# A two-layer graph network on one core: half of a dense pass replaced by gathered rows and small products

## The chip, the core and the metric

The kernel runs on one core of one Trainium2 chip, in single precision. The engines named below are TensorE (PE; its weight loads are a row of their own, PEld), VectorE (DVE), ScalarE (ACT), GpSimd (POOL) and SyncE (SP), whose queue issues most of the plain DMAs. POOL issues the indirect DMAs: one of them reads 128 row numbers from a column of an integer tile and fetches 128 rows of a DRAM table into the 128 partitions. The metric is the time of one execution on the device in microseconds; of several runs the median is given. A profile is one execution of its own, with a time span that starts at its first instruction and ends at its last.

## The reference, cut to what matters

Two layers over a graph of 3,327 nodes with 512 features each. The adjacency matrix `adj` (3,327 x 3,327) is sparse: node weights fall like one over the square root of the index, so the first rows and columns are the fullest, and the last hold a few entries in a hundred or fewer. Cut to its core:

```python
# layer 0
h = relu(layernorm(x))
u = h @ W1                      # 512 -> 128
g = relu(adj @ u + b1)          # first pass over adj
x = x + adj @ (g @ W2) + b2     # second pass: (adj @ g) @ W2
# layer 1
h = relu(layernorm(x))
t = adj @ h                                         # both sums run over the neighbours
s = exp(-leaky_relu(s_left[:, None] + s_right[None, :], 0.01)) * (adj != 0)
x_a = (s / s.sum(1)) @ (h @ W_sa)                   # attention
x_b = t @ W_gcnb + b_gcnb
own_a, own_b = h @ Wa_self + ba, h @ Wb_self + bb   # a node's own logits
x = x + sigmoid(sigmoid(t @ Wa + own_a) * x_a + sigmoid(t @ Wb + own_b) * x_b)
```

`s_left` and `s_right` are products of h with two vectors made of W_sa and a_sa. In the kernel a block's own logits are `node[i][:, 1:3]`, and its `s_left` is `node[i][:, 0:1]`.

## The kernel before, in words

Rows are padded to 3,328: 26 blocks of 128 nodes (`NB`). Seven chunks of columns of the transposed adjacency matrix (`chunks`): six of 512 and one of 256.

**First pass** (lines 493 to 537). For each chunk, 26 tiles of 128 x 512 of the adjacency matrix are loaded on SP's queue, and PE adds up `acc_u` (line 512). A product of single precision is two instructions in the profile. Beside each, DVE takes the largest magnitude of every group of 32 columns (line 516). From these, `make_lists` (line 382) writes for every block which rows of the matrix have any entry in a group of 32 columns: `row_h` holds node numbers, `row_a` row numbers of the table `adj_groups`, whose rows are 32 neighbouring columns. `list_rooms` says how many list places a block has: none for block 0, 9 for block 1, down to 5 for blocks 6 to 10, 4 for 11 to 18, 3 for 19 to 25. A place is 128 row numbers for two groups at once, and each block has two such halves: 228 columns of row numbers in all. As lists come up, `gather_adj` (line 148) fetches the pieces of the adjacency matrix into the tiles `ae`, one indirect DMA of 128 rows of 128 bytes for each column, each held back by a product that it is paced to (`gather_behind`). `make_g` ends a chunk: g of four blocks, kept in SBUF.

**Second pass** (lines 678 to 724). The same tiles are loaded again and `acc_g` is added up over all blocks of g (line 685). After a chunk, `make_h1` (line 579) makes for each of its blocks the product with W2 (`px`), the new x, its layer norm, h with its score as a row of 520 numbers (`hrow`, twelve of them in turn), the two scores (line 563), the own logits (line 567) and the store into the DRAM table `h_rows`. Block 0 is the hub, too full for lists: `add_hubs` adds up its two sums over all 26 h blocks, 52 products (line 644), beside the later chunks and after the last.

**Layer 1** (lines 767 to 987). Blocks 25 down to 1 by lists: `attend` (line 776) gathers rows of h (2,080 bytes) by `row_h` on POOL, makes the attention weights on DVE and ACT; `sums` (line 816) adds up 64 x 64 products over the gathered rows, `turn` transposes, `weigh` multiplies by the weights, `finish` (line 739) adds all up and stores. A block's gathers are paced to the sums of the third or fourth block before it (`LEAD`). If a list has no room for all rows (`overflow`), a dense path after it computes layer 1 anew; with these inputs it isn't taken.

The order on each engine is that of a scheduler at build time, by the order in the program, by readiness and by the marks `queued`, `issue_after` and `high_priority`; at run time every engine and queue runs in that order.

Of the kernel before, what the change touches and what calls it, by code (L numbers as in the profile page):

```python
# [27 lines left out]
WAKE = 14  # L28
LN_EPS = 1e-5
# [17 lines left out]
def kernel(  # L47
# [23 lines left out]
    NCH = len(chunks)  # L71
# [37 lines left out]
    s_left = [kept([P, CW // P, 2 * GW], f"s_left{c}") for c in range(NCH)]  # L109
    s_hub = kept([P, P], "s_hub")  # L110
    x1_dram = [dram.tile([P, D], F32, tag=f"x1_{i}", name=f"x1_{i}") for i in range(NB)]
    h_dram = dram.tile([NP, ROW], F32, tag="h_rows", name="h_rows")

# [16 lines left out]
    NR = 12  # L130
    rows = [
        hubp.tile([P, 2, ROW], F32, tag=f"rows{k}", name=f"rows{k}", bufs=1) for k in range(NR // 2)
    ]
    hrow = [t[:, k, :] for t in rows for k in range(2)]
    for t in rows:
        nc.vector.memset(t[:, :, D:], 0.0)

    def gather(dst, table, rows, last):
        return nc.gpsimd.indirect_dma_start(  # L139
            out=dst, out_offset=None, in_=table,  # L140
            in_offset=bass.IndirectOffsetOnAxis(ap=rows, axis=0),
            bounds_check=last, oob_is_err=False,
        )

    adj_groups = adjT.rearrange("j (b i) -> (j b) i", i=GW)
    listed = set()

    def gather_adj():

        for i in range(1, NB):  # L150
            r = rooms[i]
            for k0, k1 in segments(i):
                for q in range(2):
                    for k in range(k0, k1):
                        while (i, q) not in listed:
                            yield None
                        f = first[i] + q * r + k
                        yield gather(
                            ae[i][:, 2 * k0 + q * (k1 - k0) + k - k0, :GW], adj_groups,
                            row_a[:, f : f + 1], NP * NG - 1,  # L160
# [55 lines left out]
    with (  # L216
# [5 lines left out]
        def load_adj(j, c, name, n=1):  # L222

            c0, w = chunks[c]
            n = min(n, NB - j)
            t = adjp.tile([P, CW], F32, tag="adj", name=f"{name}_{c}_{j}")
# [33 lines left out]
        g = [l0.tile([P, HID], F32, tag=f"g{i}", name=f"g{i}") for i in range(NB)]  # L260
# [8 lines left out]
        def normalize(i):  # L269

            hs[i] = l0w.tile([P, D], F32, tag="h", name=f"h_{i}", bufs=3)
# [24 lines left out]
        def make_g(c, acc):  # L296

            c0, w = chunks[c]
            gT = l0w.tile([HID, CW], F32, tag="gT", name=f"gT_{c}")
            relu = nc.scalar.activation(gT[:, :w], acc[:, :w], AF.Relu, bias=b1_col)  # L300
            pg = bank(psB, f"pg_{c}")
            for b in range(w // P):
                nc.tensor.transpose(pg[:, b * P : (b + 1) * P], gT[:, b * P : (b + 1) * P], ident)
            for b in range(w // P):
                nc.vector.tensor_copy(g[c0 // P + b], pg[:, b * P : (b + 1) * P])
# [76 lines left out]
        def make_lists(c, most):  # L382


            c0, w = chunks[c]
            g0, n = c0 // GW, w // GW

            def small(shape, name, dtype, bufs=2):
                return l0w.tile(shape, dtype, tag=name, name=f"{name}_{c}", bufs=bufs)
# [18 lines left out]
            p_off = bank(psB, f"p_off_{c}")  # L408
# [9 lines left out]
            step = steps[c % 2]  # L418
            p_sh = bank(psB, f"p_sh_{c}")
# [14 lines left out]
            for batch in batches:  # L434
# [19 lines left out]
                for i, q in batch:  # L454
# [18 lines left out]
                nc.vector.tensor_scalar(  # L473
                    row_h[:, f0 : f0 + m], jb[:, :m], float(NP - 1), None, op0=ALU.min
                )
# [17 lines left out]
        for c in range(NCH):  # L493
            c0, w = chunks[c]
            acc = bank(psA, f"acc_u_{c}")
            per = CW // w
            most = l0w.tile([P, MG, NB], F32, tag="most", name=f"most_{c}")
            for j in range(NB):
                if c == 0:
# [8 lines left out]
                if j % per == 0:  # L508
                    with queued(x_loaded[min(j + 4, NB - 1)] if c == 0 else None):
# [5 lines left out]
                with queued(scaled[min(j + 3, NB - 1)] if c == 0 else None):  # L515
# [6 lines left out]
                if j % 3:  # L522
                    gather_behind(added)
                if c == 0 and j % 2 == 0:
# [6 lines left out]
            with tc.issue_after(chunk_end.ins):  # L531
                if c == 1:
                    load_weights()
                if 0 < c <= HUB_LOADS:
                    load_hub(c - 1)
            lists = make_lists(c, most)
# [3 lines left out]
        for s in range(2):  # L540
            a_row = l0w.tile([P, D], F32, tag="h", name=f"a_row_{s}", bufs=3)
# [12 lines left out]
            nc.vector.tensor_copy(w_rows[:, s, :], pw)  # L554

# [11 lines left out]
        def own_logits(i, junk):  # L567

            for s in range(2):
                nc.vector.scalar_tensor_tensor(  # L570
                    junk, hrow[i % NR][:, :D], 1.0, w_own[:, s, :], op0=ALU.mult, op1=ALU.mult,
                    accum_out=node[i][:, 1 + s : 2 + s],
                )
# [543 lines left out]
```

## Time and profile before

Three runs: 844.13, 844.46 and 846.61 us, median 844.46. The profiled execution's span is 840.2 us, 4.3 us below the median; around the span lies the start and end of the program.

| Engine | Busy us | Share of the span | Instructions |
|---|---|---|---|
| PE | 781.6 | 93% | 3,615 |
| PEld | 416.9 | 50% | 3,615 |
| DVE | 515.6 | 61% | 1,658 |
| ACT | 187.6 | 22% | 396 |
| POOL | 493.4 | 59% | 513 |

The first-pass products run from 11 to 220 us, those of the second pass from 220 to 434, the hub's last sums end at 457, and from 458 on layer 1 runs. In a group of the profile the columns are: busy us, mean ns of one; idle time of the engine just before them, and what ended most of it. "Issue" is a wait that the profile names no cause for. In a timeline a row is start, duration, engine, line, operation, tiles, and in brackets the idle time of the engine before it.

### The profile page before, as it was taken

The numbers are of one execution on the slowest core, as the hardware profiler recorded it, in microseconds if no ns is written. First come the engines' busy times: TensorE is split into PE (matmuls) and PEld (weight loads), VectorE is DVE, ScalarE is ACT, GpSimd is POOL, SyncE is SP. The second block draws the span as 40 slices with busy tenths as digits, with TensorE's granted clock in tenths as the row PEclk, the third lists the DMA queues.
The fourth block names the chain that finished last, engine by engine and source line by source line (L and its number), as shares of the span: only waits on it lengthen the run. The fifth ranks groups of instructions, "written<-read, shape, count | busy, mean of one in ns | idle before, by whom it ended". The sixth has DMA issues, their size and how long they took to land.

```text
span 840.2 us, 12143 instructions
## 1 busy us (share of the span) xinstructions
PE 781.6 (93%) x3615; PEld 416.9 (50%) x3615; DVE 515.6 (61%) x1658; ACT 187.6 (22%) x396; POOL 493.4 (59%) x513
## 2 busy tenths in 40 slices
PE   9999899999799999999999599799998999999795
PEld 7774344445443444444464366455554555454363
DVE  7778989999646866685775455345535353443342
ACT  7770000000002313033052022122222222121121
POOL 3202756676677777776716555666766767667400
PEclk9999999999799999999999799899999999999798
DMA  8787998898578989998958556787788867777600
GB/s 272 242 292 227 330 283 262 285 299 276 151 236 297 368 281 306 319 343 284 345 180 260 158 182 196 216 227 217 225 225 215 228 203 227 207 210 209 187 26 30
DMA packets 106891, 200.14 MB, mean 238 GB/s; under 512 B 16801, under 2 KB 30656, under 8 KB 106816
## 3 DMA queue, kind: packets, MB, share of 16 engines
q1 hardware_dynamic: 72592, 124.40, 45.2%
q0 software_dynamic: 25536, 63.74, 27.9%
q10 hardware_dynamic: 8688, 11.15, 3.8%
q8 instruction: 30, 0.49, 0.2%
q14 instruction: 45, 0.37, 0.1%
HBM read 179.39 MB, written 20.55 MB: 238 GB/s over the span
## 4 chain that ended last, share of the span: by engine, by line
PE 66%; issue 18%; DMA 7%; DVE 5%; another core or an unknown queue 3%; ACT 1%; SPq 0%; ACTq 0%; DVEq 0%
PE acc L829 14%; PE p_b L883 12%; PE p_a L890 11%; PE acc_g L685 10%; PE acc_u L512 5%; PE acc_hub L644 3%; DMA a<-in_adjT_dram 3%; PE ptt L843 3%; PE pu L291 3%; PE px L587 2%; DMA W_sa_sb<-in_W_sa_dram 1%; PE pt L283 1%; DMA xb<-in_x_dram 1%; DVE junk L563 1%
## 5 line engine op out<-in xcount | busy, mean ns | idle before, releaser
L139 POOL DMA_INDIRECT ae<-in_adjT_dram,row_a x228 | 246.4, 1081 | 151.6 <-issue 57.8
L139 POOL DMA_INDIRECT hr<-h_rows,row_h x140 | 144.1, 1029 | 64.5 <-issue 30.8
L685 PE MATMUL acc_g<-a,g 128*128 128x512 f32 (+1 forms) x364 | 160.3, 575 | 5.7 <-DMA a<-in_adjT_dram 3.8
L512 PE MATMUL acc_u<-a,rows 128*128 128x512 f32 (+1 forms) x364 | 159.9, 578 | 2.8 <-DMA a<-in_adjT_dram 2.2
L139 POOL DMA_INDIRECT rows<-h_rows,row_h x88 | 90.7, 1031 | 69.2 <-DVE e_hub L206 20.3
L883 PE MATMUL p_b<-W_g_sb,tyT 128*128 128x257 f32 x416 | 102.0, 395 | 16.3 <-issue 15.7
L516 DVE TENSOR_REDUCE most<-a 128x16 f32<-128x512 f32 (+1 forms) x182 | 110.6, 638 | 6.1 <-DMA a<-in_adjT_dram 5.2
L685 PEld LDWEIGHTS acc_g<-a,g 128*128 128x128 f32 x364 | 67.0, 192 | 85.5 <-issue 61.1
L883 PEld LDWEIGHTS p_b<-W_g_sb,tyT 128*128 128x128 f32 x416 | 78.3, 193 | 48.5 <-issue 19.3
L890 PE MATMUL p_a<-W_sa_sb,tyT 128*128 128x512 f32 (+2 forms) x216 | 97.5, 590 | 3.5 <-issue 3.1
L512 PEld LDWEIGHTS acc_u<-a,rows 128*128 128x128 f32 x364 | 66.5, 194 | 58.7 <-issue 51.9
L829 PE MATMUL acc<-hr,ae 64*64 64x512 f32 x560 | 81.7, 612 | 3.2 <-issue 2.3
L858 DVE COPY tyT<-ptt 128x512 f32<-128x512 f32 x51 | 34.9, 686 | 54.2 <-PE acc L829 21.8
L890 PEld LDWEIGHTS p_a<-W_sa_sb,tyT 128*128 128x128 f32 x216 | 41.1, 193 | 47.1 <-issue 45.6
L208 DVE SCALAR_TENSOR_TENSOR ae<-ae 128x192 f32<-128x192 f32 (+2 forms) x36 | 12.5, 368 | 79.1 <-issue 29.9
L829 PE MATMUL acc<-rows,ae 64*64 64x512 f32 x352 | 49.0, 607 | 1.7 <-issue 1.4
L829 PEld LDWEIGHTS acc<-hr,ae 64*64 64x64 f32 x560 | 30.9, 137 | 39.2 <-issue 37.9
L748 ACT ACTIVATE f<-f 128x2 f32<-128x2 f32 x26 | 5.3, 203 | 166.9 <-DVE f L747 118.4
L300 ACT ACTIVATE gT<-acc_u,b_col 128x512 f32<-128x512 f32 (+1 forms) x7 | 4.6, 657 | 157.1 <-issue 101.3
L563 DVE SCALAR_TENSOR_TENSOR junk<-rows,w_rows 128x512 bf16<-128x512 f32 x52 | 35.7, 686 | 3.0 <-issue 0.5
L716 DVE TENSOR_TENSOR xb<-xb,b_row 128x512 f32<-128x512 f32 x26 | 17.7, 689 | 30.4 <-DMA xb<-in_x_dram 19.6
L843 PEld LDWEIGHTS ptt<-ident,ty 128*128 128x128 f32 x208 | 24.5, 144 | 19.1 <-issue 18.2
(142 smaller groups left out, 907.5 us busy)
## 6 DMA issues: line engine op xcount, KB each, us to landing
a<-in_adjT_dram SPq DMA_DIRECT2D x338, 256.0 KB
h_rows<-rows SPq DMA_DIRECT2D x26, 260.0 KB
x<-in_x_dram SPq DMA_DIRECT2D x26, 256.0 KB
xb<-in_x_dram SPq DMA_DIRECT2D x26, 256.0 KB
x<-xb ACTq DMA_DIRECT2D x26, 256.0 KB
x1b<-x SPq DMA_DIRECT2D x26, 256.0 KB
out_dram<-va SPq DMA_DIRECT2D x25, 256.0 KB
ae<-in_adjT_dram,row_a POOLq DMA_INDIRECT x228
```

Of the source, the lines that this page charges most:

```text
L139: return nc.gpsimd.indirect_dma_start(out=dst, out_offset=None, in_=table, in_offset=bass.IndirectOffsetOnAxis(ap=rows, axis=0), bounds_ch ...
L291: nc.tensor.matmul(pu[:, :HID], hT[:, k, :], W1_sb[:, k, :], start=(k == 0), stop=(k == KD - 1))
L512: added = nc.tensor.matmul(acc[:, :w], u[j], a[:, :w], start=(j == 0), stop=(j == NB - 1))
L516: nc.vector.tensor_reduce(most[:, : w // GW, j], a[:, :w].rearrange("p (b i) -> p b i", i=GW), axis=AX.X, op=ALU.max, apply_absolute_value ...
L563: return nc.vector.scalar_tensor_tensor(junk, h, 1.0, w_rows[:, s, :], op0=ALU.mult, op1=ALU.mult, accum_out=into)
L644: nc.tensor.matmul(acc_hub[k], s, hrow[i % NR][:, :D], start=(i == 0), stop=(i == NB - 1))
L685: added = nc.tensor.matmul(acc[:, :w], g[j], a[:, j % per, :], start=(j == 0), stop=(j == NB - 1))
L829: added = nc.tensor.matmul(taken[i]["acc"][h][q * HALF : (q + 1) * HALF, :], both[half_p, q * n + k, :], taken[i][k0][k][half_p, q, :D], s ...
L843: moved = nc.tensor.transpose(pt[:, k * P : (k + 1) * P], ty[h][:, k * P : (k + 1) * P], ident)
L858: last = nc.vector.tensor_copy(dst, src)
L883: nc.tensor.matmul(p_b[n][:, :WH], tyT[:, k, 0, :], W_g_sb[:, k, n * WH : (n + 1) * WH], start=(k == 0), stop=(k == KD - 1),)
L890: last = nc.tensor.matmul(p_a[:, c0:c1], tyT[:, k, 1, :], W_sa_sb[:, k, c0:c1], start=(k == 0), stop=(k == KD - 1),)
```

## The change

- **Order of the first pass.** Chunks are taken from the last columns to the first (`back`): six of 512, then the 256 of blocks 0 and 1. The lists follow that order.
- **Second pass.** The last three chunks of 512, blocks 14 to 25 (`listed_chunks`), get no dense products. Their sums come from the lists: g is also stored to a DRAM table (`g_dram`), 82 indirect DMAs fetch 128 rows of 128 numbers each (`gather_g`), into four tiles of four list columns that are used in turn, and `list_sums` multiplies the pieces in `ae` by them, 64 x 32 by 64 x 128, into two PSUM banks per chunk; a copy, a transpose and a copy give sT. Blocks 0 to 13 stay dense, three chunks of 512 and one of 256 (`dense_chunks`), and the steps at which list sums are put between their products are written out (`SUMS`).
- **Making h.** `make_h1` calls for up to three of four steps instead of every second; blocks are made in the order of `made_order`, dense and listed chunks in turn; the loads of x come block by block; the hub's sums are asked for from the second dense chunk on, at every third step.
- **Own logits.** They leave the second pass. In layer 1 each block's h is loaded again (256 KB on SP's queue), and the three DVE instructions follow its `attend`.
- **Gathers of the adjacency matrix.** They follow two of three steps in both passes (one of three in the half-wide last chunk of the first); those left after the second pass are issued in layer 1, five after the gathers of each block (`AE_PER`).
- **Bounds.** No indirect DMA has a bounds check now; the lists' row numbers are clamped before `row_a` is made, which adds one small copy per batch.
- **Overflow path.** It also computes anew the listed blocks of layer 0; this code is left out below.

```diff
-    def gather(dst, table, rows, last):
+    def gather(dst, table, rows):
         return nc.gpsimd.indirect_dma_start(
             out=dst, out_offset=None, in_=table,
             in_offset=bass.IndirectOffsetOnAxis(ap=rows, axis=0),
-            bounds_check=last, oob_is_err=False,
         )
...
-                nc.vector.tensor_scalar(
-                    row_h[:, f0 : f0 + m], jb[:, :m], float(NP - 1), None, op0=ALU.min
-                )
+                nc.vector.tensor_scalar(jb[:, :m], jb[:, :m], float(NP - 1), None, op0=ALU.min)
+                nc.vector.tensor_copy(row_h[:, f0 : f0 + m], jb[:, :m])
...
-            for b in range(w // P):
-                nc.vector.tensor_copy(g[c0 // P + b], pg[:, b * P : (b + 1) * P])
+            gs = l0.tile([P, n, HID], F32, tag=f"g{c0}", name=f"g{c0}")
+            nc.vector.tensor_copy(gs, pg[:, :w].rearrange("p (b f) -> p b f", f=HID))
+            with tc.issue_after(relu.ins):
+                nc.scalar.dma_start(g_dram[c0 : c0 + w, :].rearrange("(b p) f -> p b f", p=P), gs)
...
-                if j % 3:
+                if j % 3 if w == CW else j % 3 == 0:
                     gather_behind(added)
...
+        def gather_g(n):
+            for i, f in g_slots:
+                k = len(g_taken) % NU
+                if not k:
+                    g_tile[0] = l0w.tile([P, D], F32, tag="h", name=f"g_row_{f}", bufs=GR // NU)
+                t = g_tile[0][:, k * HID : (k + 1) * HID]
+                g_taken.append(f)
+                gather(t, g_dram[:, :], row_h[:, f : f + 1])
...
+        def list_sums():
+
+            for k, (c0, w) in enumerate(listed_chunks):
+                acc = [bank(psB, f"acc_s_{c0}_{h}") for h in range(2)]
+                for b, i in enumerate(range(c0 // P, (c0 + w) // P)):
+                    r = rooms[i]
+                    for k0, k1 in segments(i):
+                        for kk in range(k0, k1):
+                            for q in range(2):
+                                t = g_rows.pop(first[i] + q * r + kk)
+                                for h in range(2):
+                                    half_p = slice(h * HALF, (h + 1) * HALF)
+                                    part = slice((2 * h + q) * GW, (2 * h + q + 1) * GW)
+                                    nc.tensor.matmul(
+                                        acc[h][part, b * P : (b + 1) * P],
+                                        ae[i][half_p, 2 * k0 + q * (k1 - k0) + kk - k0, :GW],
+                                        t[half_p, :], start=(kk == 0), stop=(kk == r - 1),
+                                    )
+                    gather_g(2 * r)
+                    yield
...
+    SUMS = (15, 22, 28, 33, 37, 42, 47, 52, 57, 62, 67, 72, 74)
...
-        for c in range(NCH):
+        gather_g(GR)
+        order = [i for c0, w in back for i in range(c0 // P, (c0 + w) // P)]
+        step = 0
+        for c, (c0, w) in enumerate(dense_chunks):
...
+                step += 1
...
+                if step in SUMS:
+                    next(summing, None)
-                if (c * NB + j) % 5 != 4:
+                if step % 3:
                     gather_behind(added)
-                if j % 2:
+                if n % 4 != 3:
...
+    def own_logits(pool, i):
+
+        own_h = pool.tile([P, D], F32, tag="own_h", name=f"own_h_{i}")
+        nc.sync.dma_start(own_h, h_dram[i * P : (i + 1) * P, :D])
...
+        def fetch_ae(n):
+            for _ in range(n):
+                with queued(gathered[0]):
+                    gathered[0] = next(columns, None) or gathered[0]
...
                 for seg in segments(i):
                     made = attend(i, seg)
...
+            with queued(made[0]):
+                own_logits(spw, i)
+            fetch_ae(AE_PER)
```

## The prediction

> **What bounds the kernel now.** I read the page first, then the busy time by stage, then the queue of GpSimd (POOL) in order of time, then one block of the last stage. The page's head and four of its groups (columns: busy us, mean ns of one; idle before, and what ended it):
>
> ```profile
> span 840.2 us, 12143 instructions
> PE 781.6 (93%) x3615; PEld 416.9 (50%) x3615; DVE 515.6 (61%) x1658; ACT 187.6 (22%) x396; POOL 493.4 (59%) x513
> ...
> L139 POOL DMA_INDIRECT ae<-in_adjT_dram,row_a x228 | 246.4, 1081 | 151.6 <-issue 57.8
> L139 POOL DMA_INDIRECT hr<-h_rows,row_h x140 | 144.1, 1029 | 64.5 <-issue 30.8
> L685 PE MATMUL acc_g<-a,g 128*128 128x512 f32 (+1 forms) x364 | 160.3, 575 | 5.7 <-DMA a<-in_adjT_dram 3.8
> L139 POOL DMA_INDIRECT rows<-h_rows,row_h x88 | 90.7, 1031 | 69.2 <-DVE e_hub L206 20.3
> ```
>
> TensorE is busy 93% of the time; POOL looks loose at 59%. By stage (stretch, its length, then busy us of PE, PEld, DVE, ACT, POOL, the clock, the DMA share, GB/s) the cuts are the end of the first tiles, of the first pass, of the second pass's products, of the hub's sums:
>
> ```profile
> 66.00:226.00 160.00, 148.35 (x789) 72.41 (x789) 141.74 (x380) 3.91 (x6) 97.86 (x96) 0.97 0.85 266
> 226.00:435.00 209.00, 202.63 (x528) 90.69 (x526) 142.26 (x468) 53.10 (x102) 148.50 (x132) 0.99 0.91 300
> 435.00:458.00 23.00, 22.03 (x54) 9.61 (x56) 12.29 (x45) 6.12 (x16) 10.18 (x11) 1.00 0.67 227
> 480.00:840.00 360.00, 331.75 (x1801) 186.83 (x1799) 161.45 (x576) 74.97 (x163) 209.73 (x204) 0.97 0.66 189
> ```
>
> PE fills 224.7 of the second pass's 232 us (226 to 458). But POOL's share hides a limit. Its queue in order of time:
>
> ```profile
> 316.57 1.00 POOL L139 DMA_INDIRECT ae<-in_adjT_dram,row_a  x1 [0.30 <-issue]
> 317.87 1.00 POOL L139 DMA_INDIRECT ae<-in_adjT_dram,row_a  x1 [0.30 <-issue]
> 319.17 1.00 POOL L139 DMA_INDIRECT ae<-in_adjT_dram,row_a  x1 [0.30 <-issue]
> ...
> 578.96 1.00 POOL L139 DMA_INDIRECT hr<-h_rows,row_h  x1 [0.30 <-issue]
> ```
>
> A gather takes 1.00 us and the next cannot follow for another 0.30: one per **1.30 us** (about 1.35 with the occasional longer one), the same for 128 bytes per index (ae) as for 2,080 (hr). In the second pass 132 gathers x 1.35 = 178 us of 209: POOL is 85% full, not 71%. Last, PE in a block of the last stage:
>
> ```profile
> 603.87 3.63 PE L829 MATMUL acc<-hr,ae 64*64 64x512 f32 x30
> 607.43 3.74 PE L883 MATMUL p_b<-W_g_sb,tyT 128*128 128x257 f32 x16
> 611.01 3.72 PE L890 MATMUL p_a<-W_sa_sb,tyT 128*128 128x512 f32 x8
> 614.56 1.04 PE L843 MATMUL ptt<-ident,ty 128*128 128x128 f32 x8
> ```
>
> PE runs without a gap: 11.7 us for a block with four list places, 10.8 for one with three (the chain of waits steps 482.1, 493.0, 503.8). A block's gathers (eight, or six) need 10.8 or 8.1 us of POOL.
>
> **What the Trainium skill says.** *DMA: Bandwidth & Descriptors*, "SWDGE vs HWDGE vs iDMA": a GpSimd DMA's descriptors are computed by software on the Q7 cores. The trace agrees: POOL's time follows the index count, not the bytes. *GPSIMD Engine Reference*, "Elementwise — side-by-side cycle accounting": data-dependent branching costs about 12 cycles per element. No run here shows it; used below. *TensorEngine Tiling (Array Packing)*, "Key Properties": tiles work independently, but changing the tiling mode drains the engine. The 30 64x64 products above take 0.121 us each, about a quarter of the 0.43 of a full 512-wide one: they do overlap. *TensorE: Matmul & The Clock Gate*, "The HAM clock gate": PE idle beyond some 3.4 us halves its clock. The trace agrees (458 to 480 us: 12.6 us busy, clock 0.77), so long waits cost twice.
>
> **The change, part by part.**
>
> *Second pass, products.* Chunks go from six and a half to three and a half: 182 products to 104, 78 of 512 columns gone. One is two instructions of 0.43 us (a run of 22 took 9.71), so 78 x 0.86 = **-67 us** of PE. Their 78 loads of 256 KB leave SP's queue and DMA share (0.91) falls; no wait depends on it then.
>
> *Second pass, list sums.* 82 lists (2 x 41 places in blocks 14 to 25) x 2 halves = 164 products of 64 rows, 32 weights, 128 columns: 328 instructions. The trace has none such. Cheapest: columns alone count, a quarter of 0.121, 10 us. Dearest: they run like transposes of 128 columns, 1.04/8 = 0.13, 43 us. I take 0.065, **+21 us**, and +2 for 12 transposes. PE's second pass becomes 224.7 - 67 + 23 = 181 us.
>
> *Second pass, gathers.* POOL gets 82 gathers of g; those of adjacency fall to two steps in three: 70 in 104 steps. They share one queue in order. Beyond the first 16, a g gather waits until PE's sums free its tile; behind it stand adjacency gathers and the next g gathers, for which PE's next sums wait. The last sums stand at step 74: by then POOL has issued 82 + 50 = 132. They start when g of the last first-pass chunk is stored, 229 us.
>
> *Bounds check.* All gathers lose their bounds check (its register move runs under the gather before and costs nothing). Its price inside the 1.00 us is shown nowhere. Bounds: nothing (1.30 stays) to all of it (0.30 left). The time is per index, and a compare with a possible skip is per-index work; 12 cycles x 128 at the skill's 1.2 GHz would be 1.28 us, more than all there is, so that price is no bound but says a check need not be small. I take the middle, 0.80, rounded up to **0.85 us**. It decides the case: 132 gathers end at 229 + 112 = 341 us, against PE at step 74 near 355 (74 products 64, sums 23, 16 px and some 18 hub products 29, small ones 7, waits 6). POOL hides if one gather takes under (355 - 229)/132 = 0.95 us.
>
> *Making h1.* Per block DVE spends 0.69 + 0.68 + 0.68 on the adds and statistics, 0.5 on small ones, 1.54 on two scores, 1.16 on the hub's e: 5.2 us. At step 78 (361 us) eight blocks are still to be made beside the last 26 half-wide products: 8 x 5.2 = 42 us, then the last two blocks and the hub sums, which took 23 us here. 361 + 42 + 23 = 426; PE alone gives 226 + 181 + 8 = 415. I take 424 for the end of the second pass, **-34 us** against 458. ACT gains up to 40 table loads of 1.28 us (more switching of Sqrt and Exp): it was busy 59 of 232 us, so they lengthen only a block's chain.
>
> *Own logits.* Two scores of 0.688 + 0.084 and an add of 0.16: 1.7 us of DVE for each of 20 blocks leaves the second pass for the last stage (six were there). 34 us more on DVE's 161 of 360; in a block it stands before the second copy to tyT, for which PE's p_b waits. That copy ended at 605.3, p_b began at 607.4: 2.1 us of slack, 1.1 where the list has three places and the sums take 2.6. Seven such blocks lose 0.6: **+5 us** rounded up; without that cover 34. The 26 reloads of 256 KB (SP) lift a DMA share of 0.66 by 6.8 MB/360 us = 19 on 189 GB/s, to 0.73: hidden.
>
> *Last stage, gathers.* About 87 adjacency gathers fit in the first pass (before: 96), 70 in the second: 71 of 228 are left, five per block over 14 blocks, ahead of the next block's h gathers on POOL. 11 x 0.85 = 9.4 us against 10.8, 13 x 0.85 = 11.1 against 11.7: hidden, with 2 us for a late start; the cover ends at 0.98 and 0.90.
>
> *First pass reversed.* The 54 list places of blocks 2 to 5 now fall beside the half-wide last chunk, where 24 did, and DVE is nearly full there (142 of 160): +6 there, -4 at the start, +2 for an added copy per batch, -3 for one wide copy of g instead of four, and 1 for stores: **+2 us**. The overflow path stays untaken.
>
> *Sum.* 840.2 + 2 - 34 + 5 + 2 = 815 us of span; the median of the runs lies 4.3 above the span: **819 us**.
>
> **The rivals.** *POOL becomes the bound* (the other side): the check costs nothing, a gather stays at 1.35. Step 74 comes at 229 + 178 = 407 us, the second pass ends near 467 (+10). In the last stage blocks cost 11 x 1.35 = 14.9 for 10.8 and 13 x 1.35 = 17.6 for 11.7: 7 x 4.1 + 7 x 5.9 = 70, less some 20 of head start. 840 + 10 + 50 + 4 = 904 us. For it: the interval never varies with the work; against: the check is per index. It decides from about 1.15 us per gather.
>
> *Halfway.* A gather takes 1.0 to 1.1, or list products cost the dear 43 us with drains between tilings, or DVE's chain of making h1 has no slack at double pace. Each gives back 15 to 35 us: 835 to 860. For it: DVE at 5.2 us per block nearly equals PE's pace. Against: DVE sheds 34 us in that stage.
>
> *The list path does nothing for the end* because the hub's tail and h rows decide when the last stage starts: then 842. Against it: that tail hangs on the last chunk's products, which come earlier.
>
> **How the numbers follow.** Forecast 0.56 (own range 800 to 833), POOL bound 0.26 (880 to 915), halfway 0.14, no effect 0.04. The runs of before spread over 0.3%, the least that this measurement can tell. Of halfway's 0.14, 0.03 end faster, 0.01 the same, 0.10 slower; of no effect's 0.04, 0.01, 0.02 and 0.01: faster 0.60, same 0.03, slower 0.37. Range 800 to 900: below it some 0.04, above it half of the POOL case.
>
> **What would show it.** Gathers of the new kernel back to back: start to start 0.85 (right), 1.30 (rival). In the second pass PE waiting on g rows at list sums means POOL or its landings; PE idle after DVE scores means the h1 chain. End of the hub's sums near 424. In the last stage, blocks of 10.8 and 11.7 us again; POOL busy beyond 90% there, and PE waiting for hr, means the gathers moved there were not hidden. List products: 328 at 0.065. The forecast fails most simply through the gather's interval.

## The result and the profile after

The changed kernel takes 977.3 us (median of four runs, 971.9 to 987.9) where the kernel before takes 844.3 (842.8 to 846.6): 1.155 times as long, 95% interval 1.149 to 1.161 (the slowest of the four, 987.9 us, is left out of this ratio). The forecast was 819 us. The profiled execution spans 973.8 us against 840.2.

The page of the changed kernel, its head and three groups (the columns are those of the prediction):

```profile
span 973.8 us, 12013 instructions
PE 788.3 (81%) x3799; PEld 419.2 (43%) x3799; DVE 516.3 (53%) x1658; ACT 191.8 (20%) x401; POOL 540.8 (56%) x595
...
L159 POOL DMA_INDIRECT ae<-in_adjT_dram,row_a x228 | 223.7, 981 | 181.1 <-issue 55.2
...
L159 POOL DMA_INDIRECT g_row<-g_rows,row_h x82 | 79.1, 965 | 43.8 <-issue 21.3
L777 PE MATMUL acc_g<-a,g 128*128 128x512 f32 (+1 forms) x208 | 97.5, 593 | 4.4 <-issue 4.3
```

The large products fell from 160.3 to 97.5 us, as forecast (-63 against -67), and yet TensorE's busy share fell from 93% to 81%: it got less to do and more to wait for. The table by stage (first pass, second pass to the hub's last sum, last stage) says where:

```profile
66.00:226.00 160.00, 153.95 (x800) 74.80 (x800) 148.34 (x404) 3.91 (x6) 88.93 (x92) 0.99 0.91 286
226.00:483.00 257.00, 189.56 (x754) 85.42 (x751) 120.15 (x382) 62.86 (x119) 154.24 (x153) 0.86 0.65 196
483.00:974.00 491.00, 380.35 (x1856) 209.66 (x1854) 198.81 (x713) 77.64 (x169) 285.47 (x294) 0.86 0.58 165
```

The first pass costs what it did. The second pass ends at 483 instead of 457 (forecast 424), with TensorE busy 190 of 257 us. The last stage takes 491 us instead of 384. The clock is 0.86 in both, where it was 0.99 and 0.96. Now POOL's queue in order of time, in the second pass:

```profile
240.23 0.94 POOL L159 DMA_INDIRECT g_row<-g_rows,row_h  x1 [0.30 <-issue]
241.48 0.94 POOL L159 DMA_INDIRECT g_row<-g_rows,row_h  x1 [0.30 <-issue]
242.72 0.94 POOL L159 DMA_INDIRECT g_row<-g_rows,row_h  x1 [0.30 <-issue]
```

Start to start 1.25 us where it was 1.30: leaving out the bounds check saved 0.05 us, and not the 0.45 that I had taken. By the prediction's own count that fells the forecast (it needed less than 0.95 us) and makes the rival's premise (POOL is the bound from about 1.15 us on) true. But the rival had 904 us, and 977 were measured. What is missing shows in TensorE's own order of time, in a block of the last stage:

```profile
610.01 4.34 PE L987 MATMUL p_b<-W_g_sb,tyT 128*128 128x257 f32 x11 [3.11 <-DVE tyT L962]
615.48 0.38 PE L987 MATMUL p_b<-W_g_sb,tyT 128*128 128x257 f32 x1 [1.14 <-issue]
618.28 0.59 PE L987 MATMUL p_b<-W_g_sb,tyT 128*128 128x257 f32 x1 [2.42 <-issue]
...
628.78 1.01 PE L994 MATMUL p_a<-W_sa_sb,tyT 128*128 128x512 f32 x1 [2.21 <-issue]
630.88 4.97 PE L994 MATMUL p_a<-W_sa_sb,tyT 128*128 128x512 f32 x7 [1.09 <-issue]
```

From 614 to 631 us TensorE's starts, weight loads included, lie 0.70 us or a multiple of it apart, with no wait recorded ("issue"). The records of semaphores tell the same: those that TensorE raises normally come within 1 us of its last product's end, here they come 6 us and more late, soon after the second pass 28 us late. I add up the longest delay at each such place (those over 1 us; two within 5 us count as one place) and call the sum **lateness**: in the last stage 141 us here, 76 in the kernel before (about 10 of that in each trace is the very end). It is a sign and not a price: it moves with the rule by which places are told apart, and about a quarter of TensorE's semaphore records are missing from the trace of before (613 of 814 are there). I call the state itself the **hold**. It appears in the later part of an unbroken run of gathers on POOL: here a run of 26, from 595 to 628 us; in the kernel before runs of 18 (444 to 468 us, the hole of 9 us in TensorE's work at 461 to 470) and 16 (517 to 538).

### The profile page after: what moved, and what is told of

Read it like the earlier page. It is cut to its first block, busy times and chain, and to the rows that moved or that the text cites. A ratio compares the mean times of both kernels' runs of the same rounds, so it can differ in the third digit from the quotient of the medians.

```text
span 973.8 us, 12013 instructions
## 1 busy us (share of the span) xinstructions
PE 788.3 (81%) x3799; PEld 419.2 (43%) x3799; DVE 516.3 (53%) x1658; ACT 191.8 (20%) x401; POOL 540.8 (56%) x595
## 4 chain that ended last, share of the span: by engine, by line
PE 69%; issue 12%; another core or an unknown queue 7%; DVE 6%; DMA 3%; ACT 1%; POOL 1%; SPq 0%; ACTq 0%; DVEq 0%; POOLq 0%
PE acc_u L540 14%; PE acc L933 13%; PE p_a L994 10%; PE p_b L987 10%; PE acc_g L777 6%; PE acc_hub L664 4%; PE ptt L947 3%; PE pu L315 2%; PE px L620 2%; DMA xb<-in_x_dram 2%; PE acc_s L736 2%; PE p_list L486 1%; DVE most L544 1%; PE pt L307 1%
## 5 line engine op out<-in xcount | busy, mean ns | idle before, releaser
L159 POOL DMA_INDIRECT ae<-in_adjT_dram,row_a x228 | 223.7, 981 | 181.1 <-issue 55.2
L159 POOL DMA_INDIRECT hr<-h_rows,row_h x140 | 136.3, 974 | 78.1 <-issue 29.2
L994 PE MATMUL p_a<-W_sa_sb,tyT 128*128 128x512 f32 (+2 forms) x216 | 109.3, 626 | 24.4 <-issue 23.4
L159 POOL DMA_INDIRECT g_row<-g_rows,row_h x82 | 79.1, 965 | 43.8 <-issue 21.3
L777 PE MATMUL acc_g<-a,g 128*128 128x512 f32 (+1 forms) x208 | 97.5, 593 | 4.4 <-issue 4.3
L933 PE MATMUL acc<-rows,ae 64*64 64x512 f32 x352 | 65.1, 697 | 13.0 <-issue 6.7
L777 PEld LDWEIGHTS acc_g<-a,g 128*128 128x128 f32 x208 | 41.1, 209 | 46.4 <-issue 41.3
L233 DVE SCALAR_TENSOR_TENSOR ae<-ae 128x192 f32<-128x192 f32 (+2 forms) x36 | 12.5, 369 | 91.4 <-ACT ae L232 65.3
L620 PE MATMUL px<-W_sb,sT 128*128 128x512 f32 x52 | 33.4, 758 | 29.5 <-DVE xb L623 16.4
L623 DVE TENSOR_TENSOR xb<-px,xb 128x512 f32<-128x512 f32 x26 | 17.4, 684 | 71.0 <-issue 56.7
L847 DVE TENSOR_TENSOR vb<-p_b,bg_row 128x257 f32<-128x257 f32 x26 | 11.0, 424 | 66.6 <-PE acc L933 31.5
```

What stands on the lines that cost most here:

```text
L159: return nc.gpsimd.indirect_dma_start(out=dst, out_offset=None, in_=table, in_offset=bass.IndirectOffsetOnAxis(ap=rows, axis=0),)
L620: last_row[2] = nc.tensor.matmul(px, sT[:, b * P : (b + 1) * P], W2_sb, start=True, stop=True)
L777: added = nc.tensor.matmul(acc[:, :w], g[j], a[:, n % per, :], start=(n == 0), stop=(n == NB - 1))
L933: added = nc.tensor.matmul(taken[i]["acc"][h][q * HALF : (q + 1) * HALF, :], both[half_p, q * n + k, :], taken[i][k0][k][half_p, q, :D], s ...
L994: last = nc.tensor.matmul(p_a[:, c0:c1], tyT[:, k, 1, :], W_sa_sb[:, k, c0:c1], start=(k == 0), stop=(k == KD - 1),)
```

## Experiments: bursts of gathers

Theory: a long burst of gathers holds TensorE back. Rivals: POOL's queue in itself (time, whatever fills it); the 128-byte rows; the own logits; the small list products; waiting for g rows. Two expectations below say "132 gathers of g": there are 82 (132 was my count of g and adjacency gathers up to step 74), and 24 in the form with one listed chunk; the adjacency gathers left for the last stage are 70. Where a text gives no interval, its time is that of one run. Two chips with the hold carry these experiments: on the first the kernel before takes 835.4 us (one run), on the second, from 320 numbers on in the spacing and in the runs marked so, 841.8 (seven runs). The trace of before that they are set against is that of the first result.

**No adjacency gathers in the last stage** (`fetch_ae` returns at once, and the emptying loop `for _ in columns` before block 1 is gone):

> The changed kernel, with the 71 gathers of adjacency rows that are left for the last stage left out (their tiles stay zero, so the last blocks' sums lack those neighbours). Long-burst theory: gathers that follow each other on POOL without a pause for more than about a dozen hold back TensorE, whose semaphores then come late; without the 71 the bursts of the last stage are 6 to 10 long as in the kernel before, the last stage takes 385 to 400 us instead of 484, and the whole about 880 us. Own-logits theory (the reload of h and its two products in the last stage are what costs): nothing changes, 970 to 980 us. Queue theory (POOL simply has too much to issue in the last stage): also about 880 us, so this run does not tell the first from the third.

869.5 us (before, on the same chip: 835.4); last stage 388 us. The own logits are cleared as the main cause: with them and without the 70 gathers the stage is within 5 us of the 384 of before. The 70 gathers on POOL cost over 100 us here (491 against 388).

**Gathers added to the kernel before**, behind those of each of the first 14 blocks; once rows of h, once adjacency rows:

```diff
+            for k in range(n):
+                with queued(gathered[0]):
+                    gathered[0] = gather(next(spare), h_dram[:, :], row_h[:, first[i] + k : first[i] + k + 1], NP - 1)
...
+            gather_more(i, 5)
```

> The kernel before, with 5 (14 blocks, 70 in all) additional gathers of h rows behind those of each of the first 14 blocks of the last stage, into spare tiles that nobody reads. Long-burst theory: bursts of 11 to 15 where there were 6 to 10, TensorE stops issuing late in each, and the last stage grows by 70 to 110 us, to 915 to 955 us in all. Queue theory: POOL has 298 gathers at 1.30 us in the last stage, 388 us against 382 that the stage takes now, so 850 to 865 us. Short-row theory (only gathers of 128-byte adjacency rows do the harm): no more than the queue theory says.

> The kernel before, with 5 additional gathers of adjacency rows (128 bytes each) behind the gathers of each of the first 14 blocks of the last stage, into small spare tiles that nobody reads. Long-burst theory and short-row theory: the last stage grows by 70 to 110 us, to 915 to 955 us in all. Queue theory: 850 to 865 us. If this one is slow and the one with h rows is not, short rows are the cause; if both are, the length of the burst.

927.0 and 935.6 us, last stages of 473 and 478, lateness 133 and 182. So the loss can be made in the kernel before, with nothing of the change but the number of gathers, and rows of 2,080 bytes do it as well as rows of 128.

**The same POOL time without gathers**: five fills in their place.

> The kernel before with 5 POOL fills of 800 numbers per partition (about 1.25 us each) where the two runs with additional gathers had 5 gathers: POOL is as busy as there, but not with gathers. Long-burst theory (gathers, not POOL's time, hold TensorE back): the last stage is not lengthened beyond what POOL's time asks for, 835 to 865 us in all, where the gathers gave 927 and 936. Queue theory (POOL's time alone): as slow as with the gathers, 915 to 945 us.

```profile
497.58 1.00 POOL L139 DMA_INDIRECT rows<-h_rows,row_h  x1 [0.30 <-issue]
498.58 4.07 POOL L782 MEMSET spare<- 128x800 f32 x5
502.81 1.01 POOL L139 DMA_INDIRECT rows<-h_rows,row_h  x1 [0.15 <-issue]
```

869.0 us, just above the range of the long-burst theory. The fills took 4.07 us for five, not the 6.25 meant: 57 us in all, where the gathers needed 91. The stage grew by 29 us for 57, where it had grown by 90 to 95 for 91, and the lateness did not grow (76). Both have a part, then: POOL's time counts, and gathers do something beyond their time.

**The changed kernel without its gathers of g**, all list products kept:

```diff
...
-                gather(t, g_dram[:, :], row_h[:, f : f + 1])
-                g_rows[f] = t
+                g_rows[f] = g[NB - 1]
```

> The changed kernel, with the 132 gathers of g rows left out; the list products are all there and read a fixed tile of g instead (so the result of the first layer is wrong for the last 12 blocks). Long-burst theory: the bursts of the second pass are gone, TensorE is not held back there, and the second pass ends at 420 to 440 us instead of 483; the adjacency gathers, no longer crowded out, are all issued before the last stage, which then takes about 390 us: 815 to 840 us in all. Small-product theory (the 328 products of 64x32 by 64x128 cost far more than their spacing): the second pass still ends at 465 to 485 us.

The second pass, and two rows of TensorE's order of time in it:

```profile
226.00:399.00 173.00, 163.46 (x757) 77.94 (x755) 121.15 (x388) 62.88 (x119) 77.49 (x72) 0.99 0.81 263
```

```profile
235.84 0.86 PE L732 MATMUL acc_s<-g,ae 64*32 64x128 f32 x24
236.63 6.28 PE L773 MATMUL acc_g<-a,g 128*128 128x512 f32 x14
```

The pass ends at 399 us, 58 before the kernel before and below the 424 forecast. 24 list products take 0.79 us until the next large one starts, 0.033 each: 11 us for all 328, near my cheap bound of 10. The drain at a change of tiling mode that the Trainium skill tells of (*TensorEngine Tiling (Array Packing)*, "Key Properties") is not to be seen beside that. So on TensorE's side the change does what it was meant to do. The last stage stayed at 487, since the pass was too short for the adjacency gathers, of which 70 were again left over: my expectation of 815 to 840 was wrong there, 888.1 measured.

**The gathers of g kept, but not waited for** (`g_rows[f] = g[NB - 1]` behind the gather):

> The changed kernel with all its gathers of g rows, but with the list products reading a fixed tile of g, so that no product waits for a gather (the first layer's result is then wrong for the last 12 blocks). Waiting theory: TensorE lost its time in the second pass waiting for g rows, and without that wait the pass ends as without the gathers, at 400 to 415 us instead of 483. Long-burst theory: the gathers hold TensorE back although it does not need them, and the pass ends at 440 to 480 us.

This ran on the second chip. The pass ends at 503 us, later than with the wait and beyond both ranges of the expectation; lateness in it 76 us against 53. TensorE's order of time shows the longest place:

```profile
284.13 5.49 PE L620 MATMUL px<-W_sb,sT 128*128 128x512 f32 x6 [29.34 <-ACT sT L810]
```

It waits 29.3 us for ScalarE's copy of a sum, and ScalarE waits for the semaphore of TensorE's own last product of that sum, which comes 28.7 us late. On these chips, then, 82 gathers whose rows no product waits for cost some 104 us (503 against 399, on two chips less than 1% apart).

**Spacing.** A small fill ahead of every gather: more work for POOL, none less. With 64 numbers, in the kernel before and the changed one:

> The kernel before, with a small POOL fill (64 numbers per partition, into a spare tile) ahead of each of the 228 gathers of the last stage: more work on POOL, no work less anywhere. Long-burst theory, in its sharper form that only gathers at their full rate (1.25 to 1.30 us each) fill something up, and that at about 1.5 us they do not: TensorE's late semaphores of the last stage go (7 to 9 us in the first block, 4 to 5 in the fifth, 2 to 5 in later ones), and the kernel gets faster by 5 to 30 us. Queue theory: POOL has more to do, so the time stays or grows by up to 20 us.

> The changed kernel with the same small fill ahead of every gather from the second pass on (about 440). Long-burst theory: although POOL needs some 80 to 110 us more in all, TensorE is not held back and the time falls from 977 to 900 to 950 us, most of it set by POOL's queue now. Queue theory: POOL's 440 gathers at about 1.5 instead of 1.245 us make it slower, 1020 to 1090 us.

843.1 and 968.1 us. Both missed their point: most of the fill hid in the 0.30 us between gathers, which came at 1.335 and 1.28 us. The lateness stayed (81 and 171). With 320 numbers, on the second chip:

> The kernel before with a larger POOL fill (320 numbers per partition, about 0.4 us) ahead of each gather of the last stage, so that they come at about 1.6 us instead of 1.30 (with 64 numbers it was 1.34, which was too little to test anything). Full-rate form of the long-burst theory: TensorE's late semaphores at 470, 540 and 625 us go (7, 7 and 5 us there); the time is set by POOL's added 70 us against what is won, 835 to 870 us. If the lateness stays as it is, what holds TensorE back is not the rate of the gathers.

```profile
462.34 1.09 POOL L148 DMA_INDIRECT hr<-h_rows,row_h  x1 [0.17 <-issue]
463.42 0.38 POOL L142 MEMSET filler<- 128x320 f32 x1
463.97 1.01 POOL L148 DMA_INDIRECT hr<-h_rows,row_h  x1 [0.17 <-issue]
```

```profile
541.69 3.74 PE L893 MATMUL p_b<-W_g_sb,tyT 128*128 128x257 f32 x16
545.26 3.59 PE L900 MATMUL p_a<-W_sa_sb,tyT 128*128 128x512 f32 x8
```

At 1.55 us the hold is gone: no semaphore of the last stage is late but at the very end, and blocks run without a gap. POOL has 57 us more to do, and the time is the same (840.7 against 841.8): what the hold had taken, the queue now takes. The stage is POOL's 354 us and 26 more.

**Shorter bursts with more work**: the added adjacency gathers again, with four fills (3.26 us) ahead of each five.

> The kernel before with the 5 additional adjacency gathers per block (14 blocks) as above, and between them and the h gathers ahead of them 4 POOL fills of 800 numbers (3.2 us, 45 us in all): the same gathers, more work on POOL, and no burst of more than 8 or so. Long-burst theory: the lateness of TensorE's semaphores in these blocks (5 to 22 us each) mostly goes, and the kernel is faster than without the rests: 890 to 925 against 936 us. Queue theory: POOL's 45 us come on top, 955 to 980 us.

951.3 us on the second chip: lateness fell from 182 to 91 us, but POOL's 46 us came on top. The two runs with and without the rests are on different chips; against each chip's own kernel before they are 110 and 100 us slower, a difference too small for two single runs. The time lies in neither range: the long-burst theory's gain did not come, and the queue theory's loss is smaller than it said. Here I began to doubt that the hold was the larger part.

**The bounds checks left out of the kernel before**:

> The kernel before with the bounds checks of all 456 gathers left out and the indices limited to the table on VectorE, as the change has it. As the changed kernel's gathers show (0.94 + 0.30 = 1.245 us against 1.30), the gathers come 0.05 us closer. Queue theory: 0 to 10 us faster. Long-burst theory: the same bursts come faster, TensorE is held back a little more, and the time grows by 5 to 30 us.

840.0 against 835.4 us in single runs, gathers at 1.25 us: no gain shows here, and a loss of half a per cent is not told from none.

**One listed chunk instead of three**:

```diff
-LISTED = 3
+LISTED = 1
...
-    SUMS = (15, 22, 28, 33, 37, 42, 47, 52, 57, 62, 67, 72, 74)
+    SUMS = (15, 22, 28, 33, 37)
...
-                if step % 3:
+                if step % 3 or step > 40:
```

> The changed kernel with one column chunk of four blocks instead of three chunks summed by lists: 24 gathers of g instead of 132 (their step list cut to five), 52 large products more, and the adjacency gathers paced behind every matmul from step 41 on so that few are left for the last stage. Long-burst theory with POOL's time counted: the second pass ends at about 450 us and the last stage takes about 390, some 845 us, with 10 us less if the second pass keeps the 10 to 15 us that one listed chunk saves TensorE: 830 to 850 us, about the kernel before. If the list sums or the own logits in themselves are what costs, a third of the loss stays: 880 to 900 us.

On the second chip, 885.7 us in the middle of four runs that spread from 874.9 to 890.0; its two fastest, 874.9 and 882.5, are 1.042 (1.034 to 1.051) times the kernel before: slower than I expected of it. In its trace, that of the slowest run, the second pass was 34 us longer than in the first trace of before, with a lateness of 16 us in it; the hold alone did not explain that.

## Experiments: a chip without the hold

Three runs meant to part hold and queue fell on another chip, where the kernel before takes 762.5 us (761.1 to 766.5) and not 835 to 847:

> The changed kernel with a POOL fill of 320 numbers ahead of each gather of the last stage alone (299 gathers, at about 1.50 us instead of 1.245): 75 us more work on POOL. If TensorE's hold is what lengthens the last stage, its late semaphores there go, and the stage takes POOL's 299 x 1.50 = 449 us and a few pauses, 455 to 475 us instead of 491: 945 to 965 us in all. If POOL's queue alone sets the stage, it gets longer, 520 to 560 us, and the whole 1005 to 1045.

> The changed kernel with one listed chunk (24 gathers of g) as before, and a POOL fill of 320 numbers ahead of every gather from the second pass on. Spacing theory: in the second pass TensorE is no longer held back at its start (it lost some 14 of 44 us there), but POOL's 165 or so gathers at 1.5 us fill it nearly; the pass ends at 455 to 475 us instead of 491, the last stage takes about 390: 845 to 865 us. If the two bounds could be had together it would be the 830 us that beat the kernel before; if spacing only moves the loss to POOL, 870 to 890 as without it.

> The kernel before with a POOL fill of 200 numbers ahead of each gather of the last stage, about 1.46 us apart. If the hold begins at one interval between 1.34 us (late semaphores as without a fill) and 1.55 us (none), this one lies near it: either a part of the lateness is left at the long bursts (470 and 540 us), or none. The time stays within 1% of the kernel before in either case, 835 to 850 us, since with 1.34 and with 1.55 us it did.

940.0, 824.8 (ratio 1.079, 1.075 to 1.083) and 792.1 us (1.037, 1.034 to 1.041). The first looks nearly like the confirmation that it was to be, 480 us for the stage and no lateness. It is none: this chip shows no lateness anywhere, not even in its second pass, where the gathers came at 1.25 us. Nor does the third say anything of the interval at which the hold begins. What they do show is the queue: on this chip a fill of 0.15 us per gather costs the kernel before 30 us, where on the others 0.25 us cost nothing.

So I ran the kernels themselves there (again another chip, of the same kind):

> The changed kernel itself. On a chip where the kernel before takes about 762 us (no hold): the second pass ends near 458 us, as in the run there whose second pass was this one, the last stage takes POOL's 299 x 1.245 = 372 us and pauses, 380 to 395 us, so 840 to 860 us, 1.10 to 1.13 times the kernel before: then POOL's queue is the larger part of the loss, and the hold the rest. If the hold were all, it would be within 3% of the kernel before there. On a chip where the kernel before takes 835 to 845 us: 970 to 985 us as first measured.

> The kernel before itself, for its trace on this chip. On a chip without the hold: no late semaphore of TensorE but at the very end, a second pass that ends at about 434 us instead of 457 and a last stage of about 327 us instead of 384. On a chip with the hold: the trace first shown, 456 and 384 us.

> The changed kernel with one listed chunk, without fills. On a chip without the hold: the second pass needs 24 + 143 gathers of 1.245 us, 208 us of POOL, and ends at 430 to 440 us, the last stage with its 15 adjacency gathers takes 330 to 340 us: 762 to 782 us, no gain on the kernel before, since POOL is full. On a chip with the hold: 875 to 890 us as measured.

The changed kernel: 873.8 us against 765.2, 1.142 times (1.138 to 1.146), a little more than expected. The kernel before came as expected, with its pass ending at 434 us and 327 us for the stage. The kernel before by stage there, then the changed one:

```profile
226.00:433.00 207.00, 205.38 (x519) 94.76 (x520) 139.22 (x466) 58.31 (x114) 151.62 (x136) 1.00 0.92 309
433.00:760.00 327.00, 313.87 (x1856) 190.71 (x1854) 174.49 (x612) 75.52 (x169) 224.73 (x219) 0.99 0.77 221
```

```profile
226.00:466.00 240.00, 186.45 (x748) 85.65 (x747) 118.04 (x377) 63.13 (x119) 156.72 (x153) 0.86 0.69 208
466.00:875.00 409.00, 343.62 (x1855) 192.74 (x1854) 203.70 (x713) 75.68 (x169) 287.33 (x293) 0.93 0.67 198
```

Without the hold the kernel before is full on TensorE (205 of 207, 314 of 327 us), and the changed one still waits. Its waits, second pass and last stage (us in total, times, longest):

```profile
PE acc_s L736 <- DMA g_row<-g_rows,row_h: 50.7, 20, 7.2
...
DVE ae L904 <- DMA hr<-h_rows,row_h: 92.8, 50, 3.6
```

The first is the wait that the prediction named as the mark of a POOL bound in the second pass. In the last stage it looked for the wrong signs: it is VectorE that waits for the rows of h (11.3 us in the kernel before there), and TensorE for ScalarE's copies (41.3 us); and POOL is 70% busy, not over 90, since the 0.30 us between gathers don't count. Yet POOL is full: from 466 us to its last gather at 841 it never pauses for more than 0.31 us between two of them. The chain that ended last says the same of this stage: some 45% of it lies on the gathers and the landing of rows of h, where in the kernel before there 93% is TensorE's products. One block of the last stage, on TensorE:

```profile
548.43 3.74 PE L987 MATMUL p_b<-W_g_sb,tyT 128*128 128x257 f32 x16
552.01 3.60 PE L994 MATMUL p_a<-W_sa_sb,tyT 128*128 128x512 f32 x8
557.06 0.66 PE L947 MATMUL ptt<-ident,ty 128*128 128x128 f32 x4 [1.46 <-ACT ty L1006]
...
559.21 2.80 PE L933 MATMUL acc<-hr,ae 64*64 64x512 f32 x24
561.94 3.74 PE L987 MATMUL p_b<-W_g_sb,tyT 128*128 128x257 f32 x16
```

548.43 to 561.94: 13.5 us for a block with three list places, which takes 10.8 where nothing is late. Eleven gathers at 1.25 us are 13.8.

The form with one listed chunk: 783.1 us, 1.025 times (1.021 to 1.028), a little above what I expected. The pass ends at 444 us (before: 433), with 17 us of waiting for g rows at its start; the stage takes 337, and no adjacency gather was left for it. No form of the change that I ran beats the kernel before.

**Last stages together.** POOL's need is the number of gathers times their median start-to-start interval, and the added fills:

| kernel | gathers x us | POOL's need | stage | over it | lateness |
|---|---|---|---|---|---|
| *chips with the hold* | | | | | |
| before | 228 x 1.303 | 297 | 384 | 87 | 76 |
| before, spaced by 320 | 228 x 1.553 | 354 | 380 | 26 | 10 |
| before, fills for gathers | 228 x 1.305 + 57 | 354 | 413 | 58 | 76 |
| before + 70 of h | 298 x 1.303 | 388 | 473 | 85 | 133 |
| before + 70 of adjacency | 298 x 1.303 | 388 | 478 | 90 | 182 |
| the same, with rests | 298 x 1.306 + 46 | 435 | 493 | 58 | 91 |
| after, no adjacency here | 228 x 1.251 | 285 | 388 | 103 | 77 |
| after | 298 x 1.251 | 373 | 491 | 118 | 141 |
| *chips without* | | | | | |
| before | 228 x 1.303 | 297 | 327 | 30 | 10 |
| before, spaced by 200 | 228 x 1.449 | 330 | 358 | 27 | 10 |
| one listed chunk | 228 x 1.254 | 286 | 337 | 51 | 9 |
| the same, spaced by 320 | 228 x 1.497 | 341 | 380 | 38 | 9 |
| after | 298 x 1.254 | 374 | 410 | 36 | 9 |
| after, spaced by 320 | 298 x 1.496 | 446 | 480 | 34 | 9 |

Without lateness (beyond the 10 us of the end) the stage is POOL's need and 26 to 38 us, in one case even on a chip with the hold. The exception, one listed chunk unspaced, is the one where POOL needs least, and there TensorE is busy 316 of its 337 us: it is the bound. With lateness 58 to 118 us come on top. The six runs that the table leaves out all have the hold, 78 to 114 us over POOL's need.

## Why the prediction was wrong

**The division of the loss.** Spans: 840.2 to 973.8 us on a chip with the hold, +134; 760.6 to 875.2 on one without, +115 (by the medians of the runs +133 and +109). So most of the loss is there without the hold. The other chip makes the kernel before 80 us faster and the changed one 99, and only these 19 of the difference go with the hold. Nor is all of the 80 and 99 lateness: 56 and 81 lie in the last stage, where the lateness is, and the rest in the two passes, where the kernel before has next to none. The hold is the larger surprise and the smaller cause. Without the two traces on a chip that lacks it I would have put most of the loss down to it.

**The step that failed** is the bounds check's price, and so the gather's interval: 0.85 us taken between bounds of 0.30 and 1.30, 1.25 measured. I chose the middle of an interval that no row of the trace narrowed, although the case hung on which side of 0.95 the value lay. What spoke for a dear check was not in the trace either: every gather has 128 row numbers, so the rows show that the time doesn't follow the bytes, and not that it follows the index count; and the 12 cycles per element that the prediction leaned on are a figure for element-wise work, which no run here shows. What followed from it:

- *Second pass, gathers.* By the prediction's own count, 132 gathers from 229 us on end at 229 + 132 x 1.25 = 394 us, and the last list sum starts at 393.8 in the trace without the hold. That they meet to the microsecond is chance: there POOL issued 126 gathers from 227 to 391 us, without a pause, at 1.30 us in the mean (some take longer than 0.94). The forecast had 341, hidden. The pass then ends at 466 there. That the rival had 467 is chance too, since it counted +10 from 458 and the measured step is +32 from that chip's own 433.
- *Last stage, gathers.* +2 forecast, hidden; measured +82 without the hold, +107 with it. The covers (0.98 and 0.90 us per gather) were taken block by block, and 1.25 lies beyond both. The rival's sum with 1.25 is 7 x (13.8 - 10.8) + 7 x (16.3 - 11.7) = 53 us. Both sums treat the other eleven blocks as if POOL had time to spare there. By the table POOL's need grows from 297 to 374 us, +77, and the stage by 82, in a queue that had hardly a pause left: that is nearly all of it.
- *POOL's slack in the kernel before.* The prediction set eight gathers against a block of 11.7 us and six against one of 10.8 and found room. The blocks with five places and more, which come last, it did not count: ten gathers at 1.30 us are 13.0, and TensorE makes such a block in 12.5. It can, because POOL runs ahead in the early blocks; in the trace without the hold POOL pauses for no more than 0.31 us between gathers from 485 us to the last at 729. So the room was spent already, and the fill of 0.15 us per gather showed it: the blocks up to the third with five places kept their 10.8, 11.7 and 12.5 us, and all of the +30 us came in the six after them. That chip's last stage is bound by TensorE, with POOL just able to follow.

**Right:** the products' -67 us (measured -63); the first pass (+2 forecast; its last product ends at 218 us, 220 before); own logits (+5 forecast; the stage with them and without the added gathers is 5 us longer with the hold, and 10 without it in the form with one listed chunk, which is not the same form); DVE's chain of making h1, which with the gathers gone let the pass end at 399. **Mis-sized, on the good side:** list sums at 11 us of TensorE instead of 21.

**The rivals.** POOL as the bound was the one that came true, given 0.26; its mechanism holds in each place. Its 904 us fell short: it had +10 us for the second pass and +50 for the last stage, where +32 and +82 were measured without the hold, since it counted the last stage by blocks; and it knew nothing of the hold. The hole at 461 to 470 us stood in the trace of before; I read it for its low clock and took it for a slow start of the stage. Halfway and no effect fell.

**Left open:** what the hold is, where between 1.34 and 1.55 us it begins, and whether chip or circumstance decides that it comes. The gathers bring it on (added gathers do, fills don't, wider spacing ends it), but only on some chips, and one rival cause is untested: the recording itself. The traces of the kernel before hold 8,393 updates of semaphores on a chip with the hold and 18,385 on one without, those of the changed kernel 7,635 and 18,924, and the records thin out from about 80 us on, long before the last stage. All runs with the hold have such thin traces (under 10,000), the spaced one that shows none of it too. Every run on record has a granted clock and a span, so none shows what these chips do unrecorded. The loss without the hold rests on full traces. Spacing the changed kernel on a chip with the hold by enough was not tried.

## What to carry to other kernels

Count the queue of gathers stage by stage as number times start-to-start interval, over the whole stage and not only for the blocks that change: here 297 us of gathers in a stage of 327 were no slack but a second bound, hidden by a busy share of 59%. Where a forecast hangs on one price that the trace doesn't show, don't settle on the middle of its bounds: work out on which side of the deciding point most of the interval lies, and let the chances say that. And before a stall is blamed for a difference, see whether the kernel before has it too.

## What the runs showed of the hardware

- An indirect gather of 128 rows occupies POOL for 0.94 us without and 1.00 with the bounds check, and the next starts 0.30 later, whether rows have 128, 512 or 2,080 bytes. A fill of 64 numbers goes partly into the 0.30 (interval 1.303 to 1.335).
- On some chips gathers 1.25 to 1.34 us apart, in runs of 16 to 26 where they were counted, make TensorE fall behind: instructions 0.70 us apart or a multiple, semaphores up to 31 us late. Of VectorE's and ScalarE's semaphores, none that was recorded came more than 1.5 us late but at the very end; about 40% of theirs are missing there (800 of 1,389 and 241 of 374 in the trace of before). At 1.55 us apart there was none of it, and fills of the same engine did not bring it on. On two other chips it never came, and the same kernel took 762 instead of 844 us.
- 24 products of 64x32 tiles with 128 columns between 128x128 products take 0.79 us from their start to the next large one.
